# The tokens' scales made on GpSimd alone, and a timetable laid out anew, in a two-layer convolution and attention kernel

## The chip, the core and the metric

The kernel runs on one core of a Trainium2 chip. Its five engines run side by side: TensorE (PE in the profile; its weight loads are PEld), VectorE (DVE), ScalarE (ACT), GpSimd (POOL) and SyncE (SP), which here only issues transfers (SPq). Each engine takes its own instructions in the order of the program and waits on semaphores for the others. The metric is the device time of one execution in microseconds: before the change 2710.05 us, the median of 3 runs (2708.84 to 2710.51).

## The reference, cut to what matters

The input x has 16 images of 256 channels and 64 × 64 pixels (4096 tokens), in float32. Two layers follow each other:

```
x = x + L0(gn(x))      # linear attention over the tokens
x = x + L1(gn(x))      # top-2 of 4 experts: depthwise 3x3, gelu, pointwise

# in L0, for each token (pixel), over the 256 channels:
rmsnorm(v) = v / max(sqrt(sum(v*v)), 1e-12) * g * sqrt(256)
qkv  = w_qkv @ rmsnorm(x);  q = softmax(q over 32), k = softmax(k over tokens)
out  = w_out @ (k v^T applied to q) + b_out
L0   = rmsnorm(out)
```

The group norm gn works per image and needs the statistics of the whole image; so does the router of L1, which picks two experts per image from the mean of its normed channels. Both rmsnorms of L0 need one number for each token: 1/sqrt of its sum of squares over 256. These numbers are the tokens' scales. The kernel calls that of the first norm r and that of the second s.

## The kernel before, in words

The kernel treats the images as a software pipeline. Four images are in work at a time. For an image b, the phase "in" loads it and takes its statistics; the phase "q" makes q, k, v and the context; "out" applies the context and adds the result; "route" chooses the experts; "x" and "v" are the experts' convolutions, x the first 128 channels on PE (through a layout made by a transfer, `lay` and `spread`) and v the others by DVE taps. The phases "in", "q" and "out" go over 8 groups g of 512 tokens (4 pieces of 128 tokens), "x" and "v" over 4 quarters j of the image.

**The order of the work** is written out by a timetable. The dictionary PLAN gives each step a place inside its phase, in units of which an image takes 64 (about 162 us in the middle of the run); entries such as `"mix_a@0.7"` replace the place of one step at one image and group (`@0.7` is image 0, group 7; `e1` is the last image, `e2` the one before). All steps of all images are sorted by their places, and each engine then executes its instructions in that order, under manual scheduling. So a place orders a step against the others on its engine, and never makes it wait by itself.

**The steps around the change**, by name and line:

- `x_squares` (ACT, L563) takes the squares of 256 channels of 128 tokens on ACT and puts their sum in one column of `tss`; four of these make the tile of a group.
- `token_scale` (step `token`) makes r (128 partitions × 4) from `tss` by the helper `rsqrt`. Its two instructions are L480, on DVE: max with 1e-24 and times 1/256; and L481, on POOL: to the power −0.5.
- r is then used by `x_keep` (DVE, L572, in images 0 and 1; ACT, L574, in the others) and by `evacuate` (exp on ACT, L595).
- `out_squares` (ACT, L689), `out_scale` (by the same helper, a tile s of 128 × 2 for each half group) and `out_norm` (ACT at L702 in images 0, 1 and 15; DVE at L704 in the others) do the same for the second norm. `out_turn` (PE, L709) and `out_add` (DVE, L718) follow.
- `rsqrt` is called at two further places, for the group norms' scale sc of an image, with 128 × 2 elements.

**What else the steps of the prediction touch:** `spread_taps` (DVE, L460) builds a table of convolution taps once, in the head of the run, in four parts of nine operations. After the context (PE, L605) of image 0 come `mix_a` (DVE, L638 and L640), `mix_turn` (PE, L646), `mix_v` (DVE, L651), `mix_vv` (PE, L657), `mix_b` (DVE, L665), `mix_out` (PE, L670) and `mix_c` (DVE, L673), each waiting for the one before; then `attend` (PE, L681). `q_norm` (POOL, L620) divides q by its sums. `choose` (from L772 on, nearly all on DVE; one power on POOL at L777) and `pick_taps`, `pick_rows` choose the experts; `rest` is its L787. `build_taps` (POOL, L865) makes tiles for PE. `tap1` (DVE, L982) is the commonest DVE instruction: 1024 times over 128 × 1024 elements, with two inputs in SBUF. `conv0` (PE, L960), `pointwise` (PE, L1009 and L1020) and `residual` (DVE, L1040) end an image's second layer. PE's results lie in seven banks of PSUM, which all steps share; a bank comes free when its last reader has run.

Of the kernel before, what the change touches and what calls it, by code (L numbers as in the profile page):

```python
# [12 lines left out]
ALU = mybir.AluOpType  # L13
# [5 lines left out]
C = 256  # L19
# [20 lines left out]
RMS_EPS2 = 1e-24  # L40
# [14 lines left out]
    "load_x1": 3.37, "mean": 1.04, "means": 3.52, "dev": 4.87, "devs": 8.89, "scale": 9.45,  # L55
    "bias": 11.52, "in_lead": 22.3, "norm0": -6.17, "norm1": -4.11, "turn_x0": 1.31, "x_sq0": 1.69,
    "x_sq1": 1.83, "turn_x1": 1.65, "x_sq2": 2.02, "x_sq3": 2.28, "token": 3.74, "x_keep0": 5.36,
    "x_keep1": 5.44, "x_keep2": 5.44, "x_keep3": 5.52, "project0": 5.44, "evacuate0": 5.54,
    "project1": 5.44, "evacuate1": 5.92, "project2": 5.91, "evacuate2": 6.64, "project3": 5.98,
    "evacuate3": 6.89, "context": 9.32, "q_sum": 9.03, "q_norm": 12, "q_turn": 16.19,  # L60
    "q_keep": 16.19, "mix_a": 10.19, "mix_turn": 11, "mix_v": 11.28, "mix_vv": 12.37,
    "mix_b": 12.82, "mix_out": 13.12, "mix_c": 13.89, "mix_lead": 15.68, "attend0": 0.06,
    "out_sq0": 0.29, "out_sq1": 0.57, "out_scale0": 2.03, "out_norm0": 2.39, "attend1": 0.36,
    "out_sq2": 1.06, "out_sq3": 1.14, "out_scale1": 2.99, "out_norm1": 3.44, "out_turn0": 5.58,
    "out_add0": 6.65, "sq_sums0": 6.71, "out_turn1": 6.03, "out_add1": 6.99, "sq_sums1": 7.28,
    "sums1": 7.76, "means1": 7.81, "scale1": 9.25, "router": 10.39, "route": 11.51, "choose": 14.5,
    "pick_taps": 14.53, "route_lead": 22.21, "pick_rows0": 14.59, "pick_rows1": 16.79,
    "pick_row_bias": 16.8, "weigh": 20.59, "pick_bias": 22.49, "pick000": 0.46, "pick100": 13.34,
    "pick001": 1.12, "pick101": 14.29, "pick002": 3.33, "pick102": 14.85, "pick003": 9.35,
    "pick103": 15.3, "pick010": 1.88, "pick110": 13.4, "pick011": 2.85, "pick111": 15.01,  # L70
    "pick012": 5.64, "pick112": 16.49, "pick013": 7.87, "pick113": 16.64, "lay_pw": 10.56,
    "spread_pw": 16.4, "taps0": 10, "taps1": -2.11, "taps2": 2.39, "taps3": 2.21, "taps4": 0.06,
    "taps5": -0.36, "taps6": 11.98, "taps7": 12.19, "pad1": -8.87, "start0": -3.66, "tap01": 0.82,
    "tap02": 1.13, "tap03": 2.63, "tap04": 3.26, "tap05": 3.77, "tap06": 4.16, "tap07": 5.2,
    "tap08": 6.9, "gelu10": 10.54, "start1": 3.48, "tap11": 6.63, "tap12": 6.96, "tap13": 8.52,
    "tap14": 10.65, "tap15": 11.96, "tap16": 12.74, "tap17": 13.13, "tap18": 14.53, "gelu11": 15.45,
    "pad00": 1.77, "pad01": 2.61, "lay": 4.89, "spread0": 7.01, "conv0": 11.4, "gelu00": 11.97,
    "spread1": 6.3, "conv1": 11.54, "gelu01": 12.04, "spread2": 8.42, "conv2": 10.47,
    "gelu02": 10.92, "spread3": 8.53, "conv3": 13.42, "gelu03": 13.66, "spread4": 11, "conv4": 13.5,
    "gelu04": 14.14, "spread5": 8.57, "conv5": 13.54, "gelu05": 14.75, "spread6": 11.13,  # L80
    "conv6": 14.12, "gelu06": 15.38, "spread7": 11.35, "conv7": 14.67, "gelu07": 15.43,
    "pw00": 17.36, "pw01": 17.6, "pw02": 18.41, "pw03": 18.51, "pw10": 19.84, "pw11": 21.82,
    "pw12": 23.01, "pw13": 23.12, "residual00": 21.14, "residual01": 25.75, "residual02": 25.99,
    "residual03": 27.83, "store0": 33.89, "residual10": 24.44, "residual11": 25.79,
    "residual12": 26.61, "residual13": 29.12, "store1": 34.17, "in_first": 2.75, "in_more": 1.5,
    "q_first": 8.89, "out_first": 16.03, "out_more": 16.9, "q_less": 0.26, "load_a0": -15,
    "load_a1": -10.99, "load_b0": -19.03, "load_b1": -9.1, "stats0": -4.82, "stats1": -2.13,
    "load_weights": 1.12, "scale_weights": -12.42, "spread_taps00": -5.35, "spread_taps01": 17.3,
    "spread_taps10": 11.76, "spread_taps11": 17.38, "end_pw00": 13.31, "end_pw01": 18.72,
    "end_pw02": 22.13, "end_pw03": 7.41, "end_residual00": 20.31, "end_residual01": 25.62,  # L90
    "end_residual02": 31.9, "end_residual03": 29.15, "end_pw10": 18.67, "end_pw11": 22.93,
    "end_pw12": 11.75, "end_pw13": 18.49, "end_residual10": 21.41, "end_residual11": 24.46,
    "end_residual12": 15.92, "end_residual13": 36.59, "x_0": -0.06, "x_1": -0.02, "x_2": -0.03,
    "x_e1": 0.54, "x_e2": 0.22, "route_0": 2.1, "route_1": -0.04, "route_2": -0.02,
    "route_e1": 2.01, "route_e2": 0.08, "out_0": -0.59, "out_1": -0.06, "out_2": 0.02,
    "out_e1": 0.11, "out_e2": 0.02, "q_0": -0.13, "q_1": 1.5, "q_2": 0.24, "q_e1": 0.04,
    "q_e2": -0.03, "in_0": -16.29, "in_1": 3.75, "in_2": 0.39, "in_e1": 0.21, "in_e2": 0.24,
    "pw04": 14.44, "pw14": 33.82, "x_last": 15.94, "v_last": 15.78, "v_e1": 1.28,
    "tap18@e2.3": 12.77, "start0@e1.3": -5.22, "token@2.7": 4.71, "pw01@e2.3": 19.93,
    "x_sq2@2.2": 2.18, "gelu11@e1.2": 14.9, "spread2@e1.3": 5.41, "tap03@0.1": 1.48,  # L100
    "tap01@2.0": 0.68, "pw13@0.3": 24.37, "project0@0.0": 3.39, "out_norm1@2.7": 4.42,
    "out_sq1@e2.0": 0.41, "end_residual13@e1.3": 33.92, "out_scale1@1.2": 2.55,
    "out_turn0@0.4": 5.97, "attend1@2.0": 1.06, "token@0.4": 3.55, "evacuate0@1.2": 5.49,
    "token@e1.6": 4.93, "context@1.7": 9.94, "pw02@e1.2": 18.01, "out_scale1@0.0": 3.4,
    "q_norm@0.0": 11.06, "spread2@e2.3": 5.47, "out_turn0@1.4": 4.71, "out_turn0@e2.4": 5.12,
    "mix_turn@0.7": 11.19, "conv4@e2.3": 13.56, "residual10@2.3": 24.68, "token@2.1": 5.3,
    "out_sq3@1.6": 1.1, "pw02@e1.1": 19.41, "project0@2.7": 5.24, "context@0.5": 9.82,
    "context@0.7": 9.42, "pw12@e2.1": 24.38, "pw12@0.3": 23.18, "attend1@e1.3": 0.68,
    "pw10@1.2": 20.9, "out_norm1@1.1": 3, "pw13@e1.2": 24.53, "pw13@e1.1": 24.14,
    "context@2.1": 11.97, "pw12@0.2": 22.61, "pw12@e2.2": 22.05, "pw02@2.2": 19.2,  # L110
    "spread2@e2.1": 5.54, "out_scale0@1.1": 2.2, "pw12@2.0": 22.71, "q_norm@0.6": 11.1,
    "out_turn0@e1.5": 4.61, "out_norm0@1.1": 2.2, "spread4@e2.3": 9.28, "gelu11@e2.3": 13.3,
    "evacuate2@1.7": 6, "out_norm1@0.6": 3.17, "pw12@e1.2": 24.21, "evacuate2@2.2": 6.34,
    "project0@2.3": 4.27, "pw02@0.2": 18.87, "token@2.2": 5.19, "mix_a@0.7": 9.42,
    "norm0@0.0": -32.28, "token@0.0": 4.16, "q_sum@0.0": 11.05, "x_sq2@2.6": 1.88,
    "pw02@e2.2": 18.05, "pw03@e2.2": 19.37, "norm1@0.0": -9.05, "spread4@e1.0": 7.83,
    "out_norm1@e1.1": 2.09, "dev@0.7": -0.03, "pw12@1.1": 22.26, "x_sq2@1.2": 1.83,
    "pw12@e1.1": 22.68, "pw13@1.0": 23.47, "tap04@e2.2": 3.13, "x_keep0@0.5": 4.83,
    "out_turn0@1.2": 6.03, "pw12@1.0": 22.94, "pw03@e2.1": 19.98, "evacuate3@1.7": 6.11,
    "out_scale1@1.6": 3.43, "residual00@e2.3": 20.18, "pw10@e1.2": 19.97, "q_sum@e2.4": 11.3,  # L120
    "x_sq2@2.5": 1.74, "pw03@e1.2": 18.65, "turn_x0@0.0": 1.65, "devs@0.7": 0.08,
    "pick010@1.0": 2.51, "pw02@e1.0": 19.56, "out_scale0@1.2": 1.96, "pw11@e2.3": 24.22,
    "pw13@2.1": 23.86, "pw13@1.1": 23.15, "pw13@0.1": 23.19, "pw02@e2.0": 19.58, "tap13@2.0": 8.96,
    "x_keep3@1.2": 5.45, "end_pw13@e1.3": 17.86, "q_sum@1.6": 10.74, "spread4@e2.0": 9.27,
    "pw02@e2.3": 19.94, "x_keep3@0.2": 6.62, "pw02@1.1": 18.79, "mix_vv@2.7": 11.67,
    "residual00@e2.2": 20.9, "pw12@1.3": 23.71, "spread_taps01@0.7": 2.37, "out_turn0@1.3": 5.81,
    "conv3@e2.0": 13.64, "q_sum@e2.6": 10.38, "pw10@2.1": 19.75, "x_sq2@0.0": 1.72,
    "pw13@e2.2": 24.41, "scale1@0.0": 9, "token@0.1": 3.09, "q_sum@1.5": 11.88,
    "spread0@e2.3": 5.05, "q_sum@1.1": 10.63, "tap12@e1.1": 6.91, "pw10@e2.2": 19.73,
    "pw10@1.1": 19.47, "pw02@2.1": 18.77, "x_keep1@0.1": 5.39, "pw12@1.2": 23.63, "q_norm@0.4": 11,  # L130
# [210 lines left out]
def pipelined_path(ctx, tc, ring, st_0, wqkv, x, w_outT, b_out, g_out, router_wT, router_b, dw, dw_b, pwT, pw_b, out):  # L341


    nc = tc.nc
# [139 lines left out]
    live = {}  # L484
# [1319 lines left out]
```

## Time and profile before

| what | number |
|---|---|
| median of 3 runs | 2710.05 us (2708.84 to 2710.51) |
| the profiled execution's own time | 2710.04 us |
| its span, first to last instruction | 2708.3 us |
| granted TensorE clock, mean | 0.994 |
| DVE: `s<-ss`, L480 | 256 instructions, 160 ns mean, 40.8 us |
| DVE: `r<-tss`, L480 | 128 instructions, 171 ns mean, 21.9 us |
| POOL: `s<-s,mhalf`, L481 | 256 instructions, 943 ns mean, 241.2 us |
| POOL: `r<-r,mhalf`, L481 | 128 instructions, 1527 ns mean, 195.4 us |
| DVE: taps, L982 | 1024 instructions, 1301 ns mean, 1323.6 us |

A row of groups names line, engine and operation, then what is written and read (out<-in, without buffer numbers), the shape, the count, the busy time and the mean duration. Instructions of one engine overlap a little, so that the sum of their durations is more than the time that they take. The idle time of an engine before an instruction is put down to the one that released it last. Times in the views of stages and in the timeline count from the first instruction.

### The profile page before, as it was taken

Reading aid. Unit: us, or ns where it says so; the run is one execution under the profiler, and the core shown is the slowest. Engines: PE = TensorE matmul, PEld = TensorE weight load, DVE = VectorE, ACT = ScalarE, POOL = GpSimd, SP = SyncE. Lnnn points to the kernel's source line nnn. Section 1 sums busy time; section 2 is a strip of 40 time slices with the busy share of each in tenths; the row PEclk is TensorE's granted clock in tenths of the full one; section 3 lists DMA queues with packets and bytes.
Section 4 is the critical chain, followed back from the end, with each engine's and each line's share of the span. In section 5 each row is a group of like instructions: output and inputs, shape, how many; then the busy total and the mean of one; then the engine's idle time right before and its main releaser. Section 6 shows DMA issues by size and latency. Waiting matters only on the chain.

```text
span 2708.3 us, 55405 instructions
## 1 busy us (share of the span) xinstructions
PE 2629.2 (97%) x19268; PEld 2258.3 (83%) x19268; DVE 2422.8 (89%) x4416; ACT 2126.3 (79%) x5326; POOL 831.5 (31%) x874
## 2 busy tenths in 40 slices
PE   6898999999999999999999999999999999998988
PEld 6777888888888888888888888888888888886867
DVE  7778898999989899898999989899898998989996
ACT  3698887887887888888887887888888887876643
POOL 3343333333333333332332333333332332422210
PEclk9999999999999999999999999999999999999999
DMA  5335454454544545454454544545454453424342
GB/s 175 102 113 152 144 160 153 141 170 142 166 150 137 169 151 161 148 151 159 148 168 138 170 149 140 168 150 162 149 145 166 146 143 121 140 101 128 132 119 99
DMA packets 229712, 394.78 MB, mean 146 GB/s; under 512 B 25904, under 2 KB 108336, under 8 KB 229424
## 3 DMA queue, kind: packets, MB, share of 16 engines
q1 hardware_dynamic: 228880, 390.75, 45.9%
q8 instruction: 156, 2.56, 0.4%
q14 instruction: 132, 1.08, 0.1%
q10 hardware_dynamic: 544, 0.39, 0.0%
HBM read 280.82 MB, written 110.23 MB: 144 GB/s over the span
## 4 chain that ended last, share of the span: by engine, by line
PE 81%; DVE 12%; ACT 3%; issue 2%; DMA 1%; POOL 1%; SPq 0%; DVEq 0%; ACTq 0%; POOLq 0%
PE pq L587 15%; PE pw L1020 14%; PE dw L960 14%; PE pw L1009 13%; PE po L681 7%; PE pc L605 7%; DVE acc L982 6%; PE tr L709 4%; PE px L556 4%; PE ptq L628 2%; DVE ring L1040 1%; DMA xr<-lay 1%; DVE ring L718 1%; DVE st L505 1%; DVE ob L704 0%
## 5 line engine op out<-in xcount | busy, mean ns | idle before, releaser
L982 DVE SCALAR_TENSOR_TENSOR acc<-pd,ds,acc 128x1024 f32<-128x1024 f32 x1024 | 1323.6, 1301 | 9.2 <-ACT acc L975 4.8
L481 POOL TENSOR_TENSOR s<-s,mhalf 128x2 f32<-128x2 f32 x256 | 241.2, 943 | 1201.8 <-DVE s L480 1143.7
L1009 PE MATMUL pw<-h,pw 128*128 128x256 f32 x2048 | 480.3, 384 | 13.5 <-DVE pw L834 5.0
L960 PE MATMUL dw<-xr,taps 128*128 128x256 f32 x2048 | 480.4, 381 | 9.9 <-DMA xr<-lay 3.8
L1020 PE MATMUL pw<-xr,psp 32*128 32x256 f32 x8192 | 480.5, 381 | 0.0
L587 PE MATMUL pq<-wqkv_n,xg 128*128 128x256 f32 x2048 | 479.3, 383 | 0.2
L1020 PEld LDWEIGHTS pw<-xr,psp 32*128 32x128 f32 x8192 | 406.4, 185 | 59.9 <-issue 37.4
L1009 PEld LDWEIGHTS pw<-h,pw 128*128 128x128 f32 x2048 | 382.4, 191 | 73.7 <-issue 18.4
L960 PEld LDWEIGHTS dw<-xr,taps 128*128 128x128 f32 x2048 | 378.1, 190 | 64.0 <-issue 8.4
L587 PEld LDWEIGHTS pq<-wqkv_n,xg 128*128 128x128 f32 x2048 | 378.9, 192 | 50.6 <-DVE ring L718 3.2
L595 ACT ACTIVATE e<-pq,r 128x256 f32<-128x256 f32 x512 | 223.1, 472 | 132.6 <-PE pq L587 117.5
L481 POOL TENSOR_TENSOR r<-r,mhalf 128x4 f32<-128x4 f32 x128 | 195.4, 1527 | 377.2 <-DVE r L480 265.1
L563 ACT ACTIVATE jx<-px 128x256 f32<-128x256 f32 x512 | 199.6, 390 | 112.0 <-PE px L556 98.2
L1040 DVE SCALAR_TENSOR_TENSOR ring<-pw,bs,ring 128x256 f32<-128x256 f32 x496 | 221.8, 475 | 64.9 <-PE pw L1009 51.2
L725 ACT ACTIVATE sqj<-ring,nm 128x512 f32<-128x512 f32 x256 | 184.9, 722 | 102.6 <-DVE ring L718 101.1
L681 PE MATMUL po<-mw,qt 128*128 128x256 f32 x1024 | 250.6, 385 | 1.5 <-DVE ring L718 0.8
L605 PE MATMUL pc<-xt,e 128*128 128x257 f32 x1024 | 245.0, 380 | 4.0 <-DVE xt L572 2.9
L968 ACT ACTIVATE xr<-dw,bv 128x256 f32<-128x256 f32 x512 | 220.8, 486 | 27.7 <-PE dw L960 27.2
L718 DVE SCALAR_TENSOR_TENSOR ring<-tr,gout,ring 128x512 f32<-128x512 f32 x256 | 189.0, 745 | 50.9 <-PE tr L709 45.2
L689 ACT ACTIVATE junk<-po 128x256 f32<-128x256 f32 x512 | 196.2, 383 | 31.1 <-PE po L681 24.3
L681 PEld LDWEIGHTS po<-mw,qt 128*128 128x128 f32 x1024 | 191.2, 192 | 30.6 <-ACT qt L631 2.1
L605 PEld LDWEIGHTS pc<-xt,e 128*128 128x128 f32 x1024 | 185.4, 190 | 27.7 <-ACT e L595 4.2
(145 smaller groups left out, 3593.6 us busy)
## 6 DMA issues: line engine op xcount, KB each, us to landing
xr<-lay SPq DMA_DIRECT2D x1024, 66.0 KB
ring<-in_x SPq DMA_DIRECT2D x256, 256.0 KB
out<-ring SPq DMA_DIRECT2D x128, 512.0 KB
xa<-in_x SPq DMA_DIRECT2D x240, 256.0 KB
xb<-in_x SPq DMA_DIRECT2D x240, 256.0 KB
lay<-pd SPq DMA_DIRECT2D x64, 594.0 KB
psp<-layp SPq DMA_DIRECT2D x128, 128.0 KB
layp<-pw SPq DMA_DIRECT2D x16, 256.0 KB
```

What stands on the lines that cost most here:

```text
L481: nc.gpsimd.tensor_tensor(out_t, out_t, mhalf[:, :n], ALU.pow)
L587: nc.tensor.matmul(pq, xg[:, k, c * P : (c + 1) * P], wqkv[:, k, : 2 * HID], start=(k == 0), stop=(k == KH - 1),)
L595: nc.scalar.activation(live["e", b, g][:, c], live["pq", b, g, c // 2][:, c % 2], AF.Exp, scale=live["r", b, g][:, c : c + 1],)
L605: nc.tensor.matmul(live["pc", b], live["e", b, g][:, c, HID:], xt[g % 2][:, c], start=(g == 0 and c == 0), stop=(g == NG - 1 and c == CG - 1),
L681: nc.tensor.matmul(po[:, c], qt[:, n * P : (n + 1) * P], live["mw", b], start=True, stop=True)
L718: nc.vector.scalar_tensor_tensor(xin, live.pop(("tr", b, g, k)), gout[:, k : k + 1], xin, ALU.mult, ALU.add, accum_out=live["sm", b][:, 0, ...
L960: nc.tensor.matmul(po, live[f"taps{g}", b][:, d * P : (d + 1) * P], rows3[:, :, d : d + W // 2], start=(d == 0), stop=(d == 1),)
L968: nc.scalar.activation(live["xr", b, j, g][:, 0 : GT // 2], po, AF.Gelu, bias=live["bv", b][:, g : g + 1])
L982: nc.vector.scalar_tensor_tensor(acc, pd1[j % 2][:, t // 3 : t // 3 + QR, t % 3 : t % 3 + W], live["ds", b][:, i, t : t + 1], acc, ALU.mul ...
L1009: nc.tensor.matmul(po[q], live["pw1", b][:, part, ms], h[:, q % 2, q // 2], start=begin, stop=end,)
L1020: nc.tensor.matmul(po[q], live["psp", b][band, g, ms], live["xr", b, j, g][band, 0 : GT // 2], start=begin and g % 4 == 0, stop=end and g ...
L1040: nc.vector.scalar_tensor_tensor(xo, po, bs, xo, ALU.add, ALU.add)
```

## The change

The helper gets a parameter for the engine of its first instruction. The two calls for r and s pass GpSimd; the calls for the group norms' scales keep VectorE. No buffer, shape or value changes.

```diff
-    def rsqrt(out_t, in_ap, op0, s0, op1, s1):
+    def rsqrt(out_t, in_ap, op0, s0, op1, s1, eng=nc.vector):
 
         n = out_t.shape[-1]
-        nc.vector.tensor_scalar(out_t, in_ap, s0, s1, op0, op1)
+        eng.tensor_scalar(out_t, in_ap, s0, s1, op0, op1)
         nc.gpsimd.tensor_tensor(out_t, out_t, mhalf[:, :n], ALU.pow)
...
         r = new(small, [P, CG], "r", b, g)
-        rsqrt(r, live.pop(("tss", b, g)), ALU.max, RMS_EPS2, ALU.mult, 1.0 / C)
+        rsqrt(r, live.pop(("tss", b, g)), ALU.max, RMS_EPS2, ALU.mult, 1.0 / C, nc.gpsimd)
...
         s = new(small, [P, 2], "s", b, g, hf)
-        rsqrt(s, live.pop(("ss", b, g, hf)), ALU.max, RMS_EPS2, ALU.mult, 1.0 / C)
+        rsqrt(s, live.pop(("ss", b, g, hf)), ALU.max, RMS_EPS2, ALU.mult, 1.0 / C, nc.gpsimd)
```

The timetable is laid out anew: of the 1185 entries of PLAN, 683 change, and 155 entries for single images are added. Most shifts are below one unit. The entries that the text below speaks of, general ones first (place before, place after):

```
token        3.74   2.59      out_scale0   2.03   0.95      out_norm0   2.39   2.52
x_sq3        2.28   1.86      out_scale1   2.99   2.44      out_norm1   3.44   3.70
residual01  25.75  25.02      residual11  25.79  26.23      out_turn0   5.58   5.57
load_a1    -10.99  -7.94      load_b0    -19.03 -17.29      load_b1    -9.10 -11.50
choose      14.50  14.63      pick_rows0  14.59  14.65      q_norm     12.00  12.08
spread0      7.01   7.03      spread1      6.30   7.92      spread2     8.42   6.36
context@0.7          9.42   9.92      mix_a@0.7            9.42  10.23
spread_taps10@0.7    3.96   3.96      spread_taps11@0.7    9.30  15.30
route_0 (shift of image 0's router)   2.10   0.63
```

## The prediction, made before the changed kernel was run

> **What bounds the kernel now.** First the page's busy shares and its chain of waits.
>
> ```profile
> PE 2629.2 (97%) x19268; PEld 2258.3 (83%) x19268; DVE 2422.8 (89%) x4416; ACT 2126.3 (79%) x5326; POOL 831.5 (31%) x874
> ...
> PE 81%; DVE 12%; ACT 3%; issue 2%; DMA 1%; POOL 1%; SPq 0%; DVEq 0%; ACTq 0%; POOLq 0%
> ```
>
> TensorE (PE) is busy 97% and carries 81% of the chain. A change that gives VectorE (DVE) time can win only where PE stands idle: 2708.3 − 2629.2 = 79.1 us. The view of stages says where that is (columns: stretch, its length, busy us of PE, PEld, DVE, ACT, POOL with their counts, granted clock, DMA share, GB/s).
>
> ```profile
> 0.00:24.00 24.00, 3.28 (x9) 2.27 (x9) 14.44 (x36) 1.28 (x1) 8.61 (x27) 1.00 0.68 209
> ...
> 79.00:100.00 21.00, 15.65 (x58) 12.00 (x59) 14.72 (x39) 7.40 (x26) 3.67 (x4) 0.76 0.34 114
> ...
> 200.00:300.00 100.00, 91.93 (x628) 76.05 (x626) 82.01 (x129) 87.95 (x225) 32.91 (x31) 0.97 0.48 147
> 300.00:2400.00 2100.00, 2089.77 (x15496) 1809.07 (x15498) 1926.77 (x3480) 1738.93 (x4316) 672.57 (x683) 1.00 0.48 151
> ...
> 2428.00:2614.00 186.00, 164.54 (x1303) 132.50 (x1303) 179.24 (x309) 108.23 (x245) 43.60 (x51) 0.97 0.40 120
> ```
>
> PE idles 20.7 us before 24 (loading, no scale yet), 5.4 in 79–100, 8.1 in 200–300, 10.2 in the whole body, 21.5 in 2428–2614 and 8 after 2700; 5 elsewhere. The body is PE's. In 2428–2614 DVE is busy 96%: there DVE is the bound, and the chain runs along its taps (L982).
>
> The timeline shows the idle stretch at 82.
>
> ```profile
> 82.33 2.55 DVE L460 SCALAR_TENSOR_TENSOR tab<-dwc,piece,tab 128x32 f32<-128x32 f32 x9
> 84.79 0.16 DVE L638 RECIPROCAL rec<-pc 128x1 f32<-128x1 f32 x1
> 84.98 0.48 DVE L640 TENSOR_SCALAR cn<-pc,rec 128x256 f32<-128x256 f32 x1
> 85.61 0.41 PE L646 MATMUL pt<-ident,cn 128*128 128x128 f32 x2 [3.45 <-DVE cn L640]
> ```
>
> PE's last context matmul ended at 82.2; rec stood behind nine tab operations. In the body the waits of PE are nearly one item, 13 times some 0.6 us, once per image, and the timeline shows how one comes about.
>
> ```profile
> PE tr L709 <- DVE ring L1040: 8.2, 13, 0.8
> ```
> ```profile
> 1150.16 0.16 DVE L480 TENSOR_SCALAR r<-tss 128x4 f32<-128x4 f32 x1
> 1150.23 0.15 DVE L772 TENSOR_TENSOR z<-pz,rb 128x4 f32<-128x4 f32 x1
> ...
> 1150.40 1.01 POOL L481 TENSOR_TENSOR r<-r,mhalf 128x4 f32<-128x4 f32 x1 [5.48 <-DVE z L772]
> ...
> 1151.37 1.05 POOL L620 TENSOR_TENSOR e<-e,qs 128x512 f32<-128x512 f32 x1
> 1151.46 0.98 DVE L787 SCALAR_TENSOR_TENSOR rest<-oh,z 128x4 f32<-128x4 f32 x1
> ...
> 1155.28 0.55 PE L709 MATMUL tr<-ident,ob 128*128 128x128 f32 x3 [0.61 <-DVE ring L1040]
> ```
>
> `rest` takes 0.98 us; `rank` (L784), the same operation on as many elements, takes 0.21. It stood still until GpSimd's e (q_norm) ended. The router's chain, the residual behind it and the transpose are late by that 0.76, and PE loses 0.61.
>
> **The operation.** 128 r and 256 s operations leave DVE. They are busy 21.9 + 40.8 = 62.7 us there, but overlap their neighbours: without them the union of DVE's instructions in the trace is 8.4 us shorter in the body and 0.80 in 2428–2614. DVE also stops waiting for ACT at them (28.7 + 14.6 us in the body, one gap of 0.79 in 2428–2614). In the body PE hides all of this: no gain from it alone.
>
> GpSimd (POOL) gains 384 tensor_scalars, which the trace has nowhere. Nearest rows: its multiplies take 0.61 us at 256 elements and 1.04 at 512 when undisturbed, so 1.7 ns an element and 0.18 fixed; a memset of one column takes 0.10, a copy of 66 columns 0.40 on average. I take 0.19, ends 0.10 and 0.40: 384 × 0.19 = 73 us, POOL 33% busy. The Trainium skill ("GPSIMD Engine Reference", Engine selection) speaks against it: elementwise work belongs on VectorE, GpSimd being about 2× slower. By that rule 2 × 0.16 = 0.32 each, 123 us and 35%: no bound either way.
>
> Latency decides more. From ACT's last sum of squares to the end of the power it is 2.43 us (s) and 2.40 (r) on average in the trace, of which DVE's queue takes 1.18 and 0.61. Now the tensor_scalar waits on POOL; behind it in that queue stand the power (which waited there before), q_norm, taps and halo copies. A second rule speaks against it ("SBUF — State Buffer", Who interferes with whom): a VectorE instruction with two SBUF inputs and a GpSimd one that reads SBUF exclude each other, the later blocking for the other's whole length. The trace agrees for POOL as the loser: the 128x2 power takes 0.70 alone and up to 1.65–1.72 under a tap. It agrees only partly for DVE: of 384 powers none lies on a slow tap (over 1.32 us); the 61 slow ones, 0.48 us each too long, all lie beside q_norm, taps or halo copies, most beside two of these back to back. By the rule, 16 added operations of 0.19 cost the DVE-bound stretch 3.0 us; by the pair rows 16 × 0.48 = 7.7; by the power's own row 0. I take 0, the row of the same 2 elements. As to latency, two waits for a tap (0.6 + 0.85), 0.19, 0.1 for the hand-over and 0.7 make 2.4: unchanged.
>
> **The timetable, by places.** Head: spread_taps11 moves from 9.3 to 15.3, behind mix_a to mix_c, so the nine tab operations leave the place ahead of rec; rec then starts at about 82.4, the transpose at 83.1 instead of 85.6: −2.5 us. DVE has room for them later (14.7 busy of 21). Clock: 0.76 over 21 us is 10.1 us at half rate, of which PE worked solidly the 5.85 from 90.63 on; without the slow spell −2.9. Does it go? PE idles of 3.7, 4.1 and 5.0 us in the trace are each followed by one; so is 226.4–229.3, with PE busy 37% of 3 us in pieces; 2487.4–2490.7, with 34%, is not. Left are an idle of about 1.0 and the mix chain, whose four matmul groups fill 2.25 of the 3.7 us after it: 48% of 4.7. Between two rows that disagree I take half, −1.5. Ends −2.5 and −6.4 (no spell, and the mix chain's matmuls sped up too). Head −4.0. PE is then full, so it carries through.
>
> 200–300: ACT is saturated at 200–216 (3.9 of every 4 us), and conv0 waits for xr's DMA. The loads slip (load_a1 −10.99 to −7.94, load_b0 −19.03 to −17.29): on SP's queue load_a1 and load_b1 now stand between image 0's spreads 2, 0 and 1. I take 0, ends −3 and +3 (the 3.7 us idle at 204.5 less or more).
>
> Body: order around choose is the same but for r. z starts 0.07 earlier, so `rest` at 1151.39. On POOL, r's tensor_scalar waits until the tap ends (1150.2), then 0.19, a hand-over and 1.01: q_norm at about 1151.45. `rest` would come first by 0.06 and the 0.61 would go; that margin is a coin's toss. All 13: −8.2; none: 0; `rest` blocked for all 1.05: +0.2 each, +2.6. I take half, −4.
>
> 2428–2614: 0.80 + 0.79 = −1.6; ends −3 (the two powers on the chain, 1.67 and 1.73, starting without DVE's queue) and +7.7. Residuals and picks trade places there without changing DVE's sum. From 2614 PE runs solid to 2699, so the saving reaches the end.
>
> Sum: −4.0 + 0 − 4 − 1.6 = −9.6 against the profiled execution's 2710.04 (span 2708.3 and 1.7 around it), which is the median 2710.05. Predicted 2700.4.
>
> **Rivals.** (1) PE hides nearly everything: only the tab operations' 2.5 and DVE's 1.6 count, the slow clock and the body's stalls stay: 2706. For it: PE 99.5% in the body. (2) Everything falls well: −6.4 −3 −8.2 −3 = −20.6: 2689.5. (3) Slower: pairs on POOL hold taps up in the DVE-bound stretch, each of 16 by 0.48, +7.7; by the same lock `rest` +2.6, the first convolution +3, less 2.5: +10.8, 2720.8. It decides as soon as a pair costs DVE more than (2.5 + 1.6 + 5.4) / 16 = 0.6 us with the other gains gone, or in the body when it eats DVE's 173 us of idle (0.56 per operation at 310). For it: the pair rows; against: no power ever slowed a tap.
>
> **Numbers.** A measurement of this kernel can tell about 0.2% (5.4 us) from no change: faster is below 2704.6, slower above 2715.5. The main case 0.56 (own range 2693 to 2704.6), (2) 0.10, (1) 0.25, (3) 0.09. So faster 0.66, same 0.25, slower 0.09. Range 2690 to 2712: it leaves out half of (2) and all of (3).
>
> **What would show it.** Right: no tab operation ahead of rec at 82, PE's idle there about 1 us, clock above 0.76 in 79–100; `tr <- ring L1040` much below 8.2; taps in 2428–2614 still 1.2–1.3; POOL's new row at 0.1–0.4; ACT end to power's end still about 2.4. Wrong: taps of 1.6 and more beside s pairs; ACT ob waiting for POOL s for more than its 9.0 us in the last image; a longer idle at 204–232; a new slow-clock spell.

## The result, and the profile after

Changed kernel: 2701.46 us (median of 7 runs, 2699.47 to 2704.21); before, on the same chip, 2708.84 us (7 runs, 2706.69 to 2713.01). Ratio 0.9969, 95% interval 0.9959 to 0.9979: faster by 8.4 us, 5.7 to 11.1. The profiled execution took 2701.51 us, its span is 2699.8. Lines below the table have moved by 39: L480 and L481 are now L519 and L520, rest L787 is L826, rank L790 is L829, the residual L1040 is L1079, the taps L982 are L1021; in the experiments a line can stand up to five further down than in before. The page's busy shares and chain:

```profile
PE 2627.1 (97%) x19268; PEld 2261.6 (84%) x19268; DVE 2363.2 (88%) x4032; ACT 2125.3 (79%) x5326; POOL 1009.4 (37%) x1258
PE 88%; DVE 7%; DMA 2%; ACT 1%; issue 1%; POOL 0%; SPq 0%; DVEq 0%; ACTq 0%; POOLq 0%
```

DVE has given up 384 instructions and 59.6 us, POOL has taken on 178 us, and DVE's share of the chain fell from 12% to 7%. The stages, with the columns of the view of before:

```profile
79.00:100.00 21.00, 17.48 (x80) 14.41 (x81) 14.87 (x39) 9.20 (x33) 4.19 (x7) 0.84 0.31 101
...
200.00:300.00 100.00, 93.43 (x636) 77.87 (x635) 81.15 (x117) 88.29 (x228) 40.66 (x47) 0.97 0.52 153
300.00:2400.00 2100.00, 2094.85 (x15568) 1816.03 (x15570) 1879.74 (x3169) 1741.17 (x4321) 824.20 (x1000) 1.00 0.50 151
2428.00:2614.00 186.00, 163.42 (x1292) 131.84 (x1289) 176.91 (x284) 106.06 (x237) 55.64 (x66) 0.96 0.42 127
```

PE's idle time falls by 1.8 us in 79–100, by 1.5 in 200–300 and by 5.1 in the body. In 2428–2614 it does not fall, although DVE is less busy there; the changed kernel is 8 to 10 us ahead by then, so that this window holds somewhat later work. The timeline at 82 shows the head:

```profile
82.38 0.15 DVE L677 RECIPROCAL rec<-pc 128x1 f32<-128x1 f32 x1
...
82.56 0.48 DVE L679 TENSOR_SCALAR cn<-pc,rec 128x256 f32<-128x256 f32 x1
...
83.10 0.44 PE L685 MATMUL pt<-ident,cn 128*128 128x128 f32 x2 [1.21 <-DVE cn L679]
```

No tab operation stands ahead of rec; the transpose comes at 83.10 instead of 85.61. In the view of waits, the wait that came once per image has halved:

```profile
PE tr L748 <- DVE ring L1079: 4.3, 11, 0.6
```

The groups of GpSimd have two new rows (shape, count, then busy us, mean ns, and the idle time before them):

```profile
L519 POOL TENSOR_SCALAR s<-ss 128x2 f32<-128x2 f32 x256 | 130.4, 509 | 1013.0 <-ACT junk L728 1010.9
L519 POOL TENSOR_SCALAR r<-tss 128x4 f32<-128x4 f32 x128 | 91.0, 711 | 315.3 <-ACT jx L602 314.6
```

Undisturbed, one takes 0.22 to 0.25 us (0.16 and 0.17 on DVE); the means are two and three times that, because 176 of the 384 take longer than 0.3 us; of these 167 begin under a tap.

**Where the time went.** I followed the same PE instructions through both traces. At the end of image 0's mix the changed kernel is 2.5 us ahead, at one of the regular stalls early on (500.80 against 503.80) 3.0, eleven images later (2282.25 against 2291.85) 9.6, at PE's end (2692.10 against 2700.39) 8.3. So: head −3.0, body −6.6, end +1.3.

For the body I took the time from image 5's context transposes to image 14's, divided by nine (the period of an image), and summed every interval between two matmuls that is more than 0.15 us above the usual one, by what follows. Times in us per image; the last column is the kernel's ratio to before in its own comparison. tr are the transposes of out_turn, px the transposes of the first norm's input (PE, L556), pq the matmuls that make q, k and v (PE, L587); the residual and ring are DVE's.

| kernel | period | tr behind the residual | px behind DVE | pq behind ring | ratio to before |
|---|---|---|---|---|---|
| before | 162.37 | 0.77 | 0.21 | 0.17 | 1 |
| changed | 161.86 | 0.52 | 0 | 0.17 | 0.9969 |
| e1: new timetable, VectorE | 172.19 | | | | 1.0634 |
| e2: old timetable, GpSimd | 161.74 | 0.39 | 0 | 0.17 | 0.9979 |
| e3: one head entry | 162.38 | 0.78 | 0.22 | 0.17 | 0.9990 |
| e5: head entry, r and s on GpSimd | 161.77 | 0.38 | 0 | 0.17 | 0.9967 |
| e6: head entry, s on GpSimd | 162.15 | 0.79 | 0 | 0.17 | 0.9976 |
| e7: head entry, r on GpSimd | 161.81 | 0.37 | 0.04 | 0.17 | 0.9979 |
| e8: e3, q_norm earlier | 162.39 | 0.76 | 0.22 | 0.19 | 0.9993 |
| e9: e5, q_norm much later | 162.51 | 0 | 0.22 | 0.39 | 0.9990 |
| e10: e3, q_norm 0.2 us later | 161.92 | 0.50 | 0.05 | 0.17 | 0.9972 |
| e11: e5, s's operation doubled | 161.81 | 0.39 | 0.07 | 0.17 | 0.9985 |
| e12: e5, q_norm in a free stretch | 161.71 | 0 | 0 | 0.39 | 0.9962 |

From before to e5 the three columns fall by 0.60 us and the period by 0.60. (The head entry is the move of spread_taps11, below.)

### The profile page after: what moved, and what is told of

Read it like the earlier page. It is cut to its first block, busy times and chain, and to the rows that moved or that the text cites. A ratio compares the mean times of both kernels' runs of the same rounds, so it can differ in the third digit from the quotient of the medians.

```text
span 2699.8 us, 55288 instructions
## 1 busy us (share of the span) xinstructions
PE 2627.1 (97%) x19268; PEld 2261.6 (84%) x19268; DVE 2363.2 (88%) x4032; ACT 2125.3 (79%) x5326; POOL 1009.4 (37%) x1258
## 4 chain that ended last, share of the span: by engine, by line
PE 88%; DVE 7%; DMA 2%; ACT 1%; issue 1%; POOL 0%; SPq 0%; DVEq 0%; ACTq 0%; POOLq 0%
PE pq L626 16%; PE pw L1059 16%; PE dw L999 15%; PE pw L1048 15%; PE po L720 8%; PE pc L644 8%; PE tr L748 4%; PE px L595 4%; DVE acc L1021 3%; PE ptq L667 2%; DMA xr<-lay 1%; DMA ring<-in_x 1%; DVE ring L1079 1%; DVE st L544 0%; DVE tab L499 0%
## 5 line engine op out<-in xcount | busy, mean ns | idle before, releaser
L1021 DVE SCALAR_TENSOR_TENSOR acc<-pd,ds,acc 128x1024 f32<-128x1024 f32 x1024 | 1310.5, 1289 | 13.1 <-ACT acc L1014 6.1
L519 POOL TENSOR_SCALAR s<-ss 128x2 f32<-128x2 f32 x256 | 130.4, 509 | 1013.0 <-ACT junk L728 1010.9
L999 PE MATMUL dw<-xr,taps 128*128 128x256 f32 x2048 | 474.9, 380 | 11.9 <-DMA xr<-lay 4.9
L1079 DVE SCALAR_TENSOR_TENSOR ring<-pw,bs,ring 128x256 f32<-128x256 f32 x496 | 223.9, 479 | 119.1 <-PE pw L1048 66.9
L520 POOL TENSOR_TENSOR s<-s,mhalf 128x2 f32<-128x2 f32 x256 | 237.6, 928 | 21.4
L613 ACT ACTIVATE xt<-px,r 128x256 f32<-128x256 f32 x448 | 180.1, 487 | 44.3 <-POOL r L520 44.3
```

Source lines behind the costliest of these rows:

```text
L520: nc.gpsimd.tensor_tensor(out_t, out_t, mhalf[:, :n], ALU.pow)
L999: nc.tensor.matmul(po, live[f"taps{g}", b][:, d * P : (d + 1) * P], rows3[:, :, d : d + W // 2], start=(d == 0), stop=(d == 1),)
L1021: nc.vector.scalar_tensor_tensor(acc, pd1[j % 2][:, t // 3 : t // 3 + QR, t % 3 : t % 3 + W], live["ds", b][:, i, t : t + 1], acc, ALU.mul ...
L1079: nc.vector.scalar_tensor_tensor(xo, po, bs, xo, ALU.add, ALU.add)
```

## Experiments

**Which part of the change makes the gain.** e1 to e4 are compared with the same runs of before.

e1, the new timetable with VectorE:

```diff
-        rsqrt(r, ..., ALU.mult, 1.0 / C, nc.gpsimd)
+        rsqrt(r, ..., ALU.mult, 1.0 / C)
-        rsqrt(s, ..., ALU.mult, 1.0 / C, nc.gpsimd)
+        rsqrt(s, ..., ALU.mult, 1.0 / C)
```

> The new timetable with both operations for r and s on VectorE again. Theory A (the engine makes the gain of the body, the timetable that of the head, and the timetable also makes the loss of the DVE-bound end): the idle at 82 is 1 us as in the changed kernel (-3 us at image 0's context), the two waits per image that went (transposes behind the residual, and px behind s on DVE) are back, about -3 + 0 + 2 = 2706 to 2709. Rival B (the timetable alone makes the gain, the engine is worth nothing): 2701 to 2703, stalls per image at 0.35 as in the changed kernel.

Measured: 2879.38 us, ratio 1.0634 (1.0619 to 1.0649). Neither theory had that. The view of DVE's waits says why:

```profile
DVE s L519 <- ACT junk L728: 192.3, 131, 6.6
DVE r L519 <- ACT jx L602: 144.4, 85, 4.0
```

In the new timetable token and out_scale0 stand about one place (2.5 us) earlier and out_scale1 half a place, close behind their sums of squares. On GpSimd, idle most of the time, that is harmless. On DVE, which works in order, s and r stop the whole queue until ACT has summed: 336.7 us of waiting, where before had 71. The two halves of the change are not independent, and the question "the timetable alone" has no answer in this form.

e2, the old timetable with GpSimd (the diff's code, PLAN of before):

> The old timetable with both operations for r and s on GpSimd: the engine change alone. Theory A: the head keeps its nine tab operations and its 2.9 us of half clock; the body gains 0.5 to 0.6 us per image (rest comes before q_norm on the shared lock, and px no longer stands behind s on DVE), -6 to -7 in all, and the end gains what leaves DVE there, 1.4 to 2.2: 2700 to 2703. Rival B: nothing of the body, 2707 to 2711. A third case: in the old order the operations stand in worse places on GpSimd, r and s come late and the time is above 2711.

Measured: 2704.16 us, ratio 0.9979 (0.9968 to 0.9990), −6.2 us. The time lies between theory A's range and rival B's; the period, 161.74 and the best of these four, is A's. A's gain of 1.4 to 2.2 us in the end did not come (see 2428–2614 below), nor did the third case.

e3, the kernel before with one entry changed:

```diff
-"spread_taps11@0.7": 9.3
+"spread_taps11@0.7": 15.3
```

> The kernel before with one entry of the timetable changed: the nine tab operations of spread_taps11 at image 0, group 7, from place 9.3 to 15.3. Theory A: the transpose after the context starts at 83.1 in place of 85.6 (-2.5) and the half-clock spell is shorter (6.8 in place of 10.2 us), -3 at the end of image 0's mix and -2.5 to -3.5 at the end, because PE is full behind it: 2705 to 2706.5. Rival: the saving is lost again before the end (PE waits for the same loads and the first convolution of image 0 at 204), 2708 to 2709.

Measured: 2706.99 us, ratio 0.9990 (0.9984 to 0.9997), −3.4 us. The transpose starts at 83.29.

e4, the changed kernel with that entry back at 9.3:

> The changed kernel with that one entry back from 15.3 to 9.3. Theory A: the transpose starts 2.5 us later, the half-clock spell is 10 us again: 2.5 to 3.5 more than the changed kernel, 2704 to 2705. Rival (the head's saving is absorbed by the waits for loads at 170 to 210): within 1 us of the changed kernel.

Measured: ratio 0.9983 (0.9975 to 0.9992), so 1.4 thousandths or 3.8 us slower than the changed kernel, whose ratio comes from another comparison. e3 and e4 bracket the head's entry from both sides.

e5, the old timetable with GpSimd and the head entry: of the 838 changed or added places of the timetable it has one.

> The old timetable with the one head entry moved and both operations on GpSimd: of the new timetable's edits only one is kept. Theory A (gain = head entry + engine; the other shifts are worth nothing or cost about 1 us): 2700 to 2702, period of an image in the body 161.74 as in the engine-only run. Rival C (the new timetable's other shifts are needed for GpSimd's queue): 2704 or more.

Measured: 2699.41 us, ratio 0.9967 (0.9955 to 0.9979), the same as the changed kernel. All the gain comes from one entry and the engine; the other shifts move nothing that this can measure. Rival C falls.

**Which operation.** e6 gives only s, e7 only r to GpSimd (as e5, with nc.gpsimd at one of the two calls).

> As the head-entry run, and only s on GpSimd; r stays on VectorE. Theory A (two per-image waits with one cause each): px no longer waits behind s on VectorE, 0.23 us per image; the choose stall stays at 0.6, since r's place on GpSimd is what delays q_norm. Period 162.37 - 0.23 = 162.14, and the DVE-bound end gains its share, 2703.5 to 2705. Rival (DVE's load as such is what counts, s being two thirds of it): two thirds of the whole, period 161.95, 2702.5 to 2703.5.

> As the head-entry run, and only r on GpSimd; s stays on VectorE. Theory A: the choose stall falls from 0.61 to about 0.23 because r's first operation on GpSimd waits for a tap and q_norm, behind it, comes after rest; px still waits behind s. Period 162.37 - 0.39 = 161.98, 2702.5 to 2704. Rival (DVE's load as such): one third, period 162.16, 2704.5 to 2705.5.

Measured: s alone 2703.22 us, ratio 0.9976 (0.9968 to 0.9984), period 162.15; r alone 2703.18 us, 0.9979 (0.9970 to 0.9987), period 161.81. The medians do not tell them apart; the periods do. r is a third of the operations and brings 0.57 of the 0.61 us; s, two thirds of them, brings 0.23, all of it at px. The rival that counted DVE's load (162.16 for r, 161.95 for s) is out by the periods. The two do not add up, since px's wait also nearly goes when r alone moves.

**Why r.** In images 3 to 15, choose's rest met q_norm (e) on GpSimd and stood still until it ended. I call this the lock, after the second rule of the prediction: such a pair does not run side by side, and the one that starts later waits for the other's end. The rows of rest and rank in before and in the changed kernel (count, then the durations in ns: least, median, most):

```profile
L787 DVE SCALAR_TENSOR_TENSOR rest<-oh,z x16: 162/976/979, 183.6 to 2572.8; 128x4 f32<-128x4 f32 x16
...
L790 DVE SCALAR_TENSOR_TENSOR rank<-rest,top,first x16: 221/223/224, 184.0 to 2573.2; 128x4 f32<-128x4 f32 x16
```
```profile
L826 DVE SCALAR_TENSOR_TENSOR rest<-oh,z x16: 161/164/165, 183.0 to 2565.6; 128x4 f32<-128x4 f32 x16
...
L829 DVE SCALAR_TENSOR_TENSOR rank<-rest,top,first x16: 223/806/810, 183.4 to 2565.9; 128x4 f32<-128x4 f32 x16
```

rest now goes first, but rank, 0.4 us behind it, reads two tiles of SBUF as well and is held 0.58 us instead. The same happened at a place that I had not looked at: weigh (DVE, L832 and L834), which multiplies an image's pointwise weights by the router's. In before's timeline q_norm starts 0.03 us ahead of one of weigh's products and holds it up (1.17 us, usually 0.34):

```profile
1010.54 1.05 POOL L620 TENSOR_TENSOR e<-e,qs 128x512 f32<-128x512 f32 x1
...
1010.57 1.17 DVE L832 TENSOR_SCALAR pw<-pw,ow 128x256 f32<-128x256 f32 x1
```

It was regular because r's power on POOL started when DVE had reached r in its queue, with z next to it: POOL was tied to DVE's step. With r's first operation on POOL the tie stays, but the distance changes. The changed kernel at the same place:

```profile
1141.98 2.47 DVE L1021 SCALAR_TENSOR_TENSOR acc<-pd,ds,acc 128x1024 f32<-128x1024 f32 x2
...
1144.02 0.53 POOL L519 TENSOR_SCALAR r<-tss 128x4 f32<-128x4 f32 x1 [5.92 <-ACT jx L602]
...
1144.37 0.15 DVE L811 TENSOR_TENSOR z<-pz,rb 128x4 f32<-128x4 f32 x1
...
1144.63 1.03 POOL L520 TENSOR_TENSOR r<-r,mhalf 128x4 f32<-128x4 f32 x1
...
1145.59 0.16 DVE L826 SCALAR_TENSOR_TENSOR rest<-oh,z 128x4 f32<-128x4 f32 x1
1145.62 0.15 POOL L978 MEMSET pd<- 128x64 f32 x1
...
1145.73 1.05 POOL L659 TENSOR_TENSOR e<-e,qs 128x512 f32<-128x512 f32 x1
...
1145.98 0.81 DVE L829 SCALAR_TENSOR_TENSOR rank<-rest,top,first 128x4 f32<-128x4 f32 x1
```

r's operation starts behind ACT's sum, under a tap, and ends 0.10 us behind that tap (1144.45). q_norm then starts 1.36 us behind z, where before has 1.14; rest starts 1.22 behind z, before 1.23. So rest is first, by 0.14 us; in e5, where q_norm follows the power at once, by 0.05.

e8 tests the lock without a change of engine: q_norm of group 0 stands ahead of r on POOL.

```diff
         own = PLAN.get(f"{key}@{nears[b]}.{g}", PLAN[key])
+        if key == "q_norm" and g == 0 and b > 2:
+            own -= 0.5
```

> As the head-entry run, r and s both on VectorE as before, but q_norm of group 0 (images 3 to 15) 0.5 place earlier, so that on GpSimd it stands ahead of r's power instead of behind it and runs some 5 us before choose. If the choose stall is the lock between q_norm and choose's small operations, rest takes 0.2 us, the stall of 0.61 goes or nearly goes without any change of engine: period 161.7 to 161.8, 2700 to 2702. If the stall has another cause (DVE simply late by its load), the period stays 162.37 and the time 2706 to 2708.

Measured: 2707.12 us, ratio 0.9993 (0.9985 to 1.0002), period 162.39: no gain, and the numbers of the other cause. Yet rest has a median of 163 ns in it. The timeline shows the reason:

```profile
1141.97 2.13 DVE L982 SCALAR_TENSOR_TENSOR acc<-pd,ds,acc 128x1024 f32<-128x1024 f32 x1
1141.97 1.05 POOL L620 TENSOR_TENSOR e<-e,qs 128x512 f32<-128x512 f32 x1
```

q_norm now meets a tap, which takes 2.13 instead of 1.28 us. DVE's last wait before the stalled transposes ends at 1141.57, 3.7 us before the router's sums pz start on PE, and from there to the end of the residual, 10.9 us, DVE has no gap above 0.04 us. In that chain 0.85 us lost on a tap costs as much as 0.81 on rest. My reading of the stall as choose's own was too narrow.

e10 leaves r and s on VectorE and only starts q_norm a little later:

```diff
+        if g < 2 and b > 2:
+            for k in range(2):
+                nc.gpsimd.memset(idle[:, 64 * k : 64 * k + 64], 0.0)
         nc.gpsimd.tensor_tensor(q4, q4, ..., ALU.mult)
```

> As the head-entry run (r and s on VectorE, old timetable, period 162.38), with two small memsets of a scratch tile (128x64 each, 0.15 us in the trace of before) on GpSimd ahead of q_norm for groups 0 and 1 of images 3 to 15: q_norm starts some 0.2 to 0.3 us later and nothing else changes. Theory D (the body's gain is a change of who comes first at the lock, not the work taken off VectorE): weigh's first product starts before q_norm and takes 0.35 instead of 1.17, rest takes 0.2 and rank 0.7, the second wait of px goes: period 161.8 to 162.0, 2702.5 to 2704. Theory E (the work taken off VectorE is what counts): period 162.37 to 162.40, 2706.5 to 2708.

Measured: 2702.67 us, ratio 0.9972 (0.9959 to 0.9984), period 161.92. Of the 0.61 us per image that both operations on GpSimd bring, 0.46 come from two memsets of 0.15 us, with all of r and s still on DVE (1923.6 us busy in the body, 1924.6 without the memsets). weigh's product now starts first:

```profile
1007.75 0.35 DVE L836 TENSOR_SCALAR pw<-pw,ow 128x256 f32<-128x256 f32 x1
1007.89 1.11 POOL L624 TENSOR_TENSOR e<-e,qs 128x512 f32<-128x512 f32 x1
1008.02 0.74 DVE L722 SCALAR_TENSOR_TENSOR ring<-tr,gout,ring 128x512 f32<-128x512 f32 x1
```

The addition behind it, with one input in PSUM, takes its usual 0.74 beside q_norm. Another of weigh's products, 5 us later, is now held up under build_taps (0.71 us), as it is in e5, so that of the 0.82 us at weigh 0.46 are kept. A change of who comes first is thus enough for most of the body's gain, without any relief of DVE (theory D). Relief counts too, at px: in e6, rest (0.98) and weigh's product (1.17) are held up as in before, and px's wait goes all the same.

**The rest of the stall.** e9 and e12 move q_norm of group 0 behind choose, from e5.

e9: q_norm also behind the next s pair, q_turn and q_keep two steps later on PE (own += 5.0 and += 1.5 for group 0, images from 3).

> As the run with the head entry and both operations on GpSimd (period 161.77), and q_norm of group 0 (images 3 to 15) moved behind choose and behind the next s pair on GpSimd, with its q_turn and q_keep two steps later on PE. If what is left of the choose stall is q_norm blocking rank for 0.5 us, rank takes 0.22 again and the stall of 0.35 (0.23 at the matmul) goes: period 161.4 to 161.5, some 3 to 4 us off, 2695.5 to 2697. If q_norm blocks a tap at the new place and VectorE has no slack there either, as with the earlier place, nothing is gained: 2699 to 2701. If the transposes of q come too late for PE: above 2702.

Measured: 2706.53 us, ratio 0.9990 (0.9984 to 0.9997), 7 us worse than e5, the number of the third case. rank takes 0.22 and the stall goes, but q_norm meets a tap again (2.08 us), px's wait of 0.22 is back, and po waits 0.36 per image, where nothing waited before. Whether po's wait comes from the moved transposes or from DVE's lateness I did not separate.

e12: q_norm held back on POOL until the addition behind the stalled transposes.

```diff
+        if g == 0 and b > 2:
+            nc.gpsimd.tensor_copy(idle[:, :1], live["sm", b - 1][:, 1, 0, 0:1])
         nc.gpsimd.tensor_tensor(q4, q4, ..., ALU.mult)
...
+        if key == "q_norm" and g == 0 and b > 2:
+            own += 1.25
```

> As the run with the head entry and both operations on GpSimd (2699.4, period 161.77), and q_norm of group 0 (images 3 to 15) behind choose on GpSimd, held back by a copy of one column that ACT writes with the sum of squares after the stalled transposes. So q_norm should run beside VectorE's additions that read PSUM and its statistics of one input, in a stretch of 2.4 us in which no VectorE instruction reads two tiles of SBUF. Theory D (what counts is which VectorE operation meets q_norm at the lock): rank takes 0.22, no other VectorE operation is longer for it, the stall of 0.35 goes, period 161.4 to 161.5 and 2695 to 2697.5. Rival (the lock's cost only moves, as in the two earlier moves): 161.7 or more, 2699 and above.

Measured: 2698.52 us, ratio 0.9962 (0.9948 to 0.9975), the lowest of all, but not apart from e5. The timeline at one image:

```profile
1305.94 0.22 DVE L793 SCALAR_TENSOR_TENSOR rank<-rest,top,first 128x4 f32<-128x4 f32 x1
...
1309.70 3.50 PE L588 MATMUL pq<-wqkv_n,xg 128*128 128x256 f32 x15 [0.23 <-DVE ring L721]
...
1310.76 0.75 DVE L721 SCALAR_TENSOR_TENSOR ring<-tr,gout,ring 128x512 f32<-128x512 f32 x1
1310.85 1.05 POOL L623 TENSOR_TENSOR e<-e,qs 128x512 f32<-128x512 f32 x1
```

The moved q_norm holds no DVE instruction up here and the stall of tr is gone, yet the period falls by 0.06 instead of 0.3. Most of the saving turned into the next wait: pq behind ring, 0.39 instead of 0.17. Theory D holds for what the lock does to rank and tr; its time was wrong, because it stopped at the first wait, and the period (161.71) is the rival's.

**The price of a pair on GpSimd.** e11 doubles s's first operation:

```diff
+        nc.gpsimd.tensor_scalar(s, ss, RMS_EPS2, 1.0 / C, ALU.max, ALU.mult)
         rsqrt(s, ss, ALU.max, RMS_EPS2, ALU.mult, 1.0 / C, nc.gpsimd)
```

> As the run with the head entry and both operations on GpSimd (2699.4), and s's tensor_scalar executed twice on GpSimd, with the same result: 256 more of 0.23 to 0.54 us. If the operation on GpSimd costs no one but GpSimd (it loses the lock against taps and is never ahead of them), the body's period stays 161.77 within 0.1 and the time within 1.5 us: 2698.5 to 2701. If each pair holds VectorE up, as the slower rival of the prediction has it with 0.48 us in the VectorE-bound end: 16 in the last image, half of them or more showing, 4 to 8 us more: 2703 to 2707.

Measured: 2705.32 us, ratio 0.9985 (0.9977 to 0.9993), 6 us slower than e5; the size is the rival's, the cause is not. The period is unchanged, 161.81. From image 15's context to PE's end it is 285.20 us, where e5 has 279.70. DVE's taps there are no longer than in e5 (180.5 us against 181.2). The path is latency: one s of the last image is ready only 5.7 us after ACT's sum, since it stands on GpSimd behind another's power (1.73), and its own two operations (1.01 and 1.11) and its power (1.60) are long too; PE's transposes wait for ob.

```profile
2502.16 0.84 ACT L703 ACTIVATE ob<-po,s 128x256 f32<-128x256 f32 x2 [3.13 <-POOL s L481]
...
2502.69 0.84 PE L710 MATMUL tr<-ident,ob 128*128 128x128 f32 x2 [2.44 <-ACT ob L703]
...
2503.46 4.97 PE L1021 MATMUL pw<-xr,psp 32*128 32x256 f32 x64
```

In the last image PE waits 3.9 us for ob, in e5 not at all; the slower clock behind the longest of these waits adds 1.2 (last section). The mean latency of s alone does not tell this: it is 3.48 us in e11's last image and 2.21 in e5's, but 3.30 in before's, where PE waits only 0.4 us for ob and the path is 278.75. What costs here is one s that comes late where PE has nothing else to do. (The two traces differ by 3.1 us more between images 1 and 2, where single executions scatter as much.)

## Why the prediction was right, and where only its sum was

2700.4 was predicted and 2701.46 measured; as a gain, 9.6 against 8.4 (5.7 to 11.1). The mechanisms of the head and of the lock were right. Three of the terms missed, and that their errors cancelled is luck.

**Head, −4.0: about −3.** The order of the tab operations was read rightly: 83.10 against a predicted 83.1 (82.73 to 84.99 in the eleven traces with the entry, 85.61 to 86.99 in the three without). e3 gives −3.4 and e4 3.8. The half given to the clock was close for the spell of the changed kernel's trace (6.8 us at half rate instead of 10.2; granted clock 0.84 instead of 0.76 in 79–100), but that is one execution: the three traces without the entry all have a spell of 10.2 us there, and of the eleven with it eight have none, two 3.4. So the question "does it go?" has a clearer answer than a half, mostly yes; why the medians still gain only 3 to 4 us I did not separate. The changed kernel's trace has another spell of 3.4 us at 177.3, which before has not; the prediction named that as a way to be wrong, without a price.

**The operation.** The price of 0.19 us was near for the undisturbed operation (0.22 to 0.25). Its row was to stand at 0.1 to 0.4; its means are 0.51 and 0.71, with the taps, and GpSimd is 37% busy instead of 33%. "Latency unchanged at 2.4" failed, in the good direction: s is ready after 1.68 us on average, r after 2.17. The sum of two waits for a tap was too high: the trace shows the first operation often free (median 0.23 us for s). The wait on DVE's queue, 1.18 us, fell to 0.16. That latency matters at the end only (e11).

The row of the Trainium skill that spoke against the change ("GPSIMD Engine Reference", Engine selection) puts elementwise work on VectorE and gives GpSimd about twice the time for operations with two inputs, but roughly line rate for one. This operation has one, so that the prediction's 2 × 0.16 does not follow from the row: undisturbed it took 0.23 against 0.16 us. It decided nothing here, since GpSimd had 63% of its time to spare.

**Body, −4: −6.6.** The −4 was half of a coin's toss between nothing and 8.2. "`rest` would come first by 0.06": it did, in all images (by 0.05 in e5 and 0.14 in the changed kernel, where a memset stands between), but the prediction stopped at rest. rank, which also reads two tiles, was next; so 0.25 of the 0.77 us per image went, some 3.3 us of the 8.2. Two steps were missing, and they bring about the other half. "In the body PE hides all of this: no gain from it alone" was wrong by 0.23 us per image, as e6 shows: the wait of px behind DVE is too short for the view of waits to list each time (it names 1.1 us, 2 times), and only the intervals between matmuls show it. And weigh's collisions with q_norm are in DVE's queue as well (e10). The cause was the right one, the lock; its places were not all found.

Here the other rule bears directly ("SBUF — State Buffer", Who interferes with whom): the page says that the order of issue, not the kind of operation, decides who blocks. The trace agrees for both orders: q_norm 0.03 us ahead of weigh's product makes it 1.17 us; 0.14 behind, 0.35 (e10). Taken strictly, the rule would have had me list every DVE instruction with two SBUF inputs within 1 us of each q_norm, and rank and weigh's sums (L834) would have been on the list. weigh's first product (L832) has one tensor and a column of scalars as inputs and is held up too; why, these runs do not show.

**200–300, 0.** PE's idle time fell by 1.5 there and rose by 0.9 in 100–200; inside the ends of 3.

**2428–2614, −1.6: about 0.** The 0.80 and the 0.79 left DVE as put: between the same two PE events (2464.2 and 2581.9 before) s's rows fall from 1.45 us busy and 0.79 waiting to none. But DVE's waits for PE grew by 1.78 (before ring<-tr) and 1.27 (before the residual), and weigh and dt were held up by the tiles that POOL builds (taps<-wv) for 1.35 more. In e5 and e2 the path from image 15's context to PE's end is 279.70 and 279.02; in the five with s on VectorE in the old order (before, e8, e10, e3, e7) it is 278.75, 278.77, 280.24, 280.46 and 280.78. So such equal kernels scatter by 2.0, and neither −1.6 nor the +1.3 of the two traces can be told from nothing.

**Rivals.** (1), PE hides nearly everything: its 2706 is about the 2706.99 of e3, which is the head without the engine; for the whole change it and (2), 2689.5, lie outside the interval. (3), pairs slow taps down: refuted in its cause. The changed kernel has 36 taps over 1.32 us where before had 61, and only 3 of them lie beside one of the added operations; with 256 more of these, e11 has 61 where e5 has 60. A slower end by way of GpSimd does exist, through the latency of s.

## What to carry to other kernels

When two engines hold each other up like this, an operation's move can be worth less for its busy time than for the order in which the instructions behind it now meet: list the instructions of the one engine that take the lock within a microsecond of each long one of the other, and follow a saved wait until the queue next stands idle, for it may be lost on the next instruction or the next wait. A timetable belongs to its choice of engines: a place that is harmless on an idle engine can stop a full one that works in order. Where a sum of small terms comes out right, check the terms by events common to both traces before believing the reasons.

## What the runs showed of the hardware

- A GpSimd tensor_scalar of 128 × 2 or 128 × 4 takes about 0.23 us, the power behind it 0.71 and 1.03; begun under a VectorE tap, such an operation ends only after the tap has (r above: 0.53 us, 0.10 behind the tap's end; a power of s in e11: 1.73 us, 0.58 behind it). Two dependent ones follow each other after 0.08 us.
- A GpSimd memset of 128 × 64 takes 0.15 us; 52 of them, two ahead of each of 26 q_norms, lengthened no VectorE instruction in the stretches of e10 that I read.
- After PE had waited 2.44 us in e11, its next 64 small matmuls took 4.97 us, where they take 3.74 in the changed kernel's body; the granted clock was 0.62 in 2503–2507. With the slower clock this wait of 2.4 us cost 3.7.
- The same rest took 0.98 us when q_norm started 0.09 us before it and 0.16 when q_norm started 0.14 us behind it; DVE additions with an input in PSUM took their usual 0.74 and 0.75 beside q_norm (e10, e12).
